# A routed FFN on one NeuronCore: the last four of 56 tiles put behind a branch on the number of tiles in use

## The chip, the cores and the metric

The kernel runs on one core of a Trainium2 chip. The metric is the device time of one execution in microseconds, as the median of several runs; lower is better. A profile is one further execution, recorded by the hardware profiler. Its line numbers are those of the kernel before, unless a line says otherwise.

## What is computed

Two layers of a graph network follow each other, each made of a graph convolution and a feed-forward part, over 6250 nodes of 256 features. The change lies in the feed-forward part of the first layer, a mixture of eight experts with two chosen per token:

```python
logits = xt @ Wr + br
probs = softmax(logits)
top_p, top_idx = top_k(probs, 2)
weights = top_p / top_p.sum(axis=-1, keepdims=True)
xn = (xt - mu) * rsqrt(var + LN_EPS)
xe = xn[None] * ln_g[:, None] + ln_b[:, None]
h = gelu(einsum('end,edh->enh', xe, W1) + b1[:, None])   # D = 256, H = 1024
y = einsum('enh,ehd->end', h, W2) + b2[:, None]
out = (weights[:, :, None] * y_of_the_two_chosen).sum(axis=1)
```

All of it is float32. The part after it (the second layer's graph sum) starts from `x + out`.

## The kernel before

The 6250 tokens are padded to 6272, 49 blocks of 128, and each has two experts, so 12544 (token, expert) pairs are computed. `routed_ffn` (line 494) does it in three stages.

*Ranking* (lines 511 to 589). Every pair gets a place, sorted by expert. Each expert's places are rounded up to whole tiles of 256 (`TS`), and `end` (line 529) is the running sum of the experts' tiles, so its last column is the number of tiles in use. How many that is depends on the data; the program is built for the largest number possible:

```python
TT = (2 * NP + n_exp * (TS - 1)) // TS      # 56
```

`te` (line 542) holds each tile's expert, `gi` the rows to gather for each place, and `so` the row of the result table `tab_y` for each place. A place that holds no pair has an `so` far out of bounds, so its row is not written, and an unused tile takes the last expert's weights.

*Tiles* (lines 591 to 654). For each tile, `start_tile` (line 592) reads its expert from `te` into a register of SP, and starts the loads of that expert's parameters (`pa`), weights (`w1` and `w2`, 1 MB each) and bias (`bb`) on SP's queue, and two gathers of 128 tokens on POOL's (line 606). This runs two tiles ahead. `turn` (line 611) transposes the gathered rows on TensorE and applies the expert's layer norm on VectorE (line 618). The tile itself is 16 matmuls with `w1` (line 630), eight Gelus on ScalarE (633), 16 matmuls with `w2` (643) in two halves, each with an addition of the bias on VectorE (645) and a scatter to `tab_y` on POOL (646). In the profile each float32 matmul is two, each with a weight load of its own. The transposes of the next tile stand between a tile's two groups of matmuls.

Beside the tiles runs other work that the second layer needs: an iterator, `beside`, of which every tile draws four steps (line 651) and the end of the loop whatever is left (653). Its steps sort the second layer's edges (`sorted_edges`, line 1453) and prepare the runs of the graph sum (`runs_of`, line 1577). They use VectorE, TensorE for transposes, ScalarE for copies, and SP's queue for loads and stores, such as the edge weights (1592) and the products `wab_d` (1642).

*Gather-back* (lines 655 to 662). The table `tab_y` is loaded in seven pieces on SP's queue (658), and VectorE adds the two rows of each token, times their gates, to `X` (661, 98 operations). Then a branch on another flag (lines 2170 and 2172) leads into the second layer.

The order on each engine is the program's order of issue, slightly rearranged by the framework's scheduler; waits between engines are on semaphores that it places. When a pool is closed and its room is taken by the next, the next one's writers wait for the last readers. A branch is loaded and taken by each engine for itself: a register load, then a compare and branch.

Of the kernel before, what the change touches and what calls it, by code (L numbers as in the profile page):

```python
# [22 lines left out]
I32 = mybir.dt.int32  # L23
I16 = mybir.dt.int16
AF = mybir.ActivationFunctionType
OP = mybir.AluOpType
AX = mybir.AxisListType
PSUM = bass.MemoryType.PSUM
# [4 lines left out]
P = 128  # L33
# [14 lines left out]
def chunks(n, size):  # L48
    return [(i, min(size, n - i)) for i in range(0, n, size)]
# [22 lines left out]
def tile_kernel(ctx, tc, src_ins, out):  # L72
    nc = tc.nc
# [420 lines left out]
    def routed_ffn(keep, tab_x, sel, gates, par_d, pre, beside):  # L494
# [5 lines left out]
        n_exp, _, HD = W1.shape  # L500
        FC = HD // P
        TS = 2 * P
        TT = (2 * NP + n_exp * (TS - 1)) // TS
# [4 lines left out]
        gi = keep.tile([P, SC], I32, name="gi")  # L508
        so = keep.tile([P, SC], I32, name="so")
        te = keep.tile([P, TT], I32, name="te")  # L510
        with tc.tile_pool(name="rk", bufs=1) as p, tc.tile_pool(name="rkw", bufs=4) as wp, \
                tc.tile_pool(name="rk_ps", bufs=1, space=PSUM) as pp:
            inc = p.tile([P, NT, n_exp], F32, name="inc")
            for e in range(n_exp):
                nc.vector.tensor_tensor_scan(inc[:, :, e], sel[:, :, e], sel[:, :, e], 0.0,
                                             op0=OP.add, op1=OP.max)
# [7 lines left out]
            end = p.tile([P, n_exp], F32, name="end")  # L524
# [15 lines left out]
            tb = p.tile([P, TT], F32, name="tb")  # L540
            nc.vector.tensor_reduce(tb, ge, AX.X, OP.add)
            nc.vector.tensor_copy(te, tb)


            all_e = [P, NT, n_exp]
# [29 lines left out]
            for i in range(2 * NT):  # L575
# [5 lines left out]
                                        op0=OP.is_equal, op1=OP.mult)  # L581
# [6 lines left out]
            nc.vector.tensor_scalar(gi, lf, 0.0, None, op0=OP.max)  # L588
            nc.vector.tensor_single_scalar(gi, gi, 1, op=OP.arith_shift_right)

        with tc.tile_pool(name="ff", bufs=3) as fp, tc.tile_pool(name="ff_ps", bufs=2, space=PSUM) as pp:
            def start_tile(j):
                _, (e,) = nc.values_load_multi_w_load_instructions(
                    te[0:1, j:j + 1], engines=[mybir.EngineType.SP], min_val=0, max_val=n_exp - 1,
                    skip_runtime_bounds_check_because="a count of n_exp-1 comparisons on chip")
                pa = fp.tile([P, NPAR], F32, name="pa")
                nc.sync.dma_start(pa, par_d[bass.ds(e, 1)].rearrange("e p c -> p (e c)"))
                w1 = fp.tile([P, KD, HD], F32, name="w1")
                nc.sync.dma_start(w1, W1[bass.ds(e, 1)].rearrange("e (k p) f -> p (e k) f", p=P))
                w2 = fp.tile([P, FC, D], F32, name="w2")  # L600
                nc.sync.dma_start(w2, W2[bass.ds(e, 1)].rearrange("e (c p) d -> p (e c) d", p=P))
                bb = fp.tile([P, D], F32, name="bb")
                nc.sync.dma_start(bb, b2[bass.ds(e, 1)].to_broadcast([P, D]))
                xg = fp.tile([P, 2, D], F32, name="xg")
                for i in range(2):
                    nc.gpsimd.indirect_dma_start(  # L606
                        out=xg[:, i, :], out_offset=None, in_=tab_x,
                        in_offset=bass.IndirectOffsetOnAxis(ap=gi[:, 2 * j + i:2 * j + i + 1], axis=0))
                return pa, w1, w2, bb, xg

            def turn(pa, xg):
                pt = pp.tile([P, KD, TS], F32, name="pt", bufs=1)
                for k in range(KD):
                    for i in range(2):
                        nc.tensor.transpose(pt[:, k, i * P:(i + 1) * P], xg[:, i, k * P:(k + 1) * P], ident)  # L615
                xe = fp.tile([P, KD, TS], F32, name="xe")
                for k in range(KD):
                    nc.vector.tensor_scalar(xe[:, k], pt[:, k], pa[:, FC + k:FC + k + 1],  # L618
                                            pa[:, FC + KD + k:FC + KD + k + 1], op0=OP.mult, op1=OP.add)
                return xe  # L620

            ahead = [start_tile(j) for j in range(2)]
            xe = turn(ahead[0][0], ahead[0][4])
            for j in range(TT):
                pa, w1, w2, bb, _ = ahead.pop(0)
                hs = []
                for f in range(FC):
                    ph = pp.tile([P, TS], F32, name="ph", bufs=4)
                    for k in range(KD):
                        nc.tensor.matmul(ph, w1[:, k, f * P:(f + 1) * P], xe[:, k, :],  # L630
                                         start=(k == 0), stop=(k == KD - 1))
                    h = fp.tile([P, TS], F32, name="h", bufs=2 * FC)
                    nc.scalar.activation(h, ph, AF.Gelu, bias=pa[:, f:f + 1])
                    hs.append(h)
                if j + 2 < TT:
                    ahead.append(start_tile(j + 2))
                if j + 1 < TT:
                    xe = turn(ahead[0][0], ahead[0][4])
                y = fp.tile([P, 2, D], F32, name="y")
                for i in range(2):  # L640
                    py = pp.tile([P, D], F32, name="py")
                    for f in range(FC):
                        nc.tensor.matmul(py, hs[f][:, i * P:(i + 1) * P], w2[:, f, :],  # L643
                                         start=(f == 0), stop=(f == FC - 1))
                    nc.vector.tensor_add(y[:, i, :], py, bb)
                    st = nc.gpsimd.indirect_dma_start(
                        out=tab_y, out_offset=bass.IndirectOffsetOnAxis(ap=so[:, 2 * j + i:2 * j + i + 1], axis=0),
                        in_=y[:, i, :], in_offset=None, bounds_check=2 * NP - 1, oob_is_err=False)
                    tc.declare_no_dep(st.ins, group="tab_y", reason="each place has a row of its own")
                    tc.add_to_no_dep_group("tab_y", st.ins)  # L650
                for _ in range(4):
                    next(beside, None)
            for _ in beside:
                pass
        with tc.tile_pool(name="fy", bufs=2) as fp:
            for t0, n in chunks(NT, CH):
                y = fp.tile([P, CH, 2 * D], F32, name="yy")
                nc.sync.dma_start(y[:, :n], tab_y[2 * t0 * P:2 * (t0 + n) * P].rearrange("(t p k) d -> p t (k d)", p=P, k=2))
                for t in range(t0, t0 + n):
                    for k in range(2):  # L660
                        nc.vector.scalar_tensor_tensor(X[:, t, :], y[:, t - t0, k * D:(k + 1) * D], g2[:, t, k:k + 1],
                                                       X[:, t, :], op0=OP.mult, op1=OP.add)
# [20 lines left out]
    class Head:  # L683
# [25 lines left out]
        def ffn(self, keep, beside):  # L709
            routed_ffn(keep, self.tab_x, self.sel, self.gates, self.par_d, "L0_ffn", beside)  # L710
# [1514 lines left out]
```

## Time and profile before

| what | value |
|---|---|
| median of 3 runs (lowest, highest) | 7773.18 us (7765.84, 7774.26) |
| the profiled execution's own time | 7783.37 us |
| its span | 7781.5 us |
| mean granted TensorE clock | 0.717 of full speed |
| busy over the span: PE, VectorE, ScalarE, POOL | 49%, 57%, 15%, 53% |
| first and last matmul of line 630 | 2784.8 and 3621.9 us |
| first load of tab_y (line 658) | 3632.38 us |
| last weighted add (line 661) begins | 3687.1 us |

A row by stretch gives the stretch, its length, then the busy time and number of instructions of each engine (PE is TensorE's matmuls, PEld its weight loads, DVE VectorE, ACT ScalarE, POOL GpSimd), the granted clock, the DMA engines' busy share and what they moved. A row of the timeline gives start, length, engine, line, operation, output and input, and in brackets the idle time before and what ended it. A row of waits gives who waited for what: total time, times, longest. A row of one line's instructions gives their number and the shortest, middle and longest duration in ns. A row of a DMA queue gives packets, MB and share of the engines' time. SPq, PEldq and the like are the engines' sequencers.

### The profile page before, as it was taken

The numbers are of one execution on the slowest core, as the hardware profiler recorded it, in microseconds if no ns is written. First come the engines' busy times: TensorE is split into PE (matmuls) and PEld (weight loads), VectorE is DVE, ScalarE is ACT, GpSimd is POOL, SyncE is SP. The second block draws the span as 40 slices with busy tenths as digits, with TensorE's granted clock in tenths as the row PEclk, the third lists the DMA queues.
The fourth block names the chain that finished last, engine by engine and source line by source line (L and its number), as shares of the span: only waits on it lengthen the run. The fifth ranks groups of instructions, "written<-read, shape, count | busy, mean of one in ns | idle before, by whom it ended". The sixth has DMA issues, their size and how long they took to land. (4 is left out here: it accounts for less than half of the span.)

```text
span 7781.5 us, 62325 instructions
## 1 busy us (share of the span) xinstructions
PE 3827.1 (49%) x17463; PEld 2901.2 (37%) x17463; DVE 4464.9 (57%) x10655; ACT 1161.1 (15%) x2758; POOL 4096.1 (53%) x4320
## 2 busy tenths in 40 slices
PE   3345545555445599996135555655555651111111
PEld 2234434444334378885023333433343431111111
DVE  4345555555555673443566666776676615665666
ACT  2011111111111112321001222212221210000000
POOL 0666666666666322321566666666566445555552
PEclk9667777777777799998557777777777875555555
DMA  4444444444444245565433333333333212222221
GB/s 124 119 114 119 113 117 120 117 119 118 115 114 120 73 163 190 184 228 167 139 89 99 98 103 100 101 102 102 95 100 101 80 43 52 45 48 52 50 50 41
DMA packets 496232, 821.82 MB, mean 106 GB/s; under 512 B 143344, under 2 KB 315587, under 8 KB 495842
## 3 DMA queue, kind: packets, MB, share of 16 engines
q0 software_dynamic: 190880, 462.26, 22.4%
q1 hardware_dynamic: 292326, 343.79, 14.5%
q10 hardware_dynamic: 12668, 11.68, 0.5%
q8 instruction: 141, 2.31, 0.1%
q14 instruction: 217, 1.78, 0.1%
HBM read 743.27 MB, written 77.29 MB: 105 GB/s over the span
## 5 line engine op out<-in xcount | busy, mean ns | idle before, releaser
L234 POOL DMA_INDIRECT g<-tab_ef,si x1616 | 1537.3, 951 | 995.4 <-issue 557.9
L1260 POOL DMA_INDIRECT g<-tab,si x1612 | 1539.6, 955 | 924.5 <-issue 577.4
L2028 DVE SCALAR_TENSOR_TENSOR run<-g,wab,run 128x256 f32<-128x256 f32 x2626 | 1264.9, 488 | 551.0 <-remote 179.2
L1260 POOL DMA_INDIRECT g<-tab_1f,si1s x787 | 761.8, 968 | 666.3 <-issue 587.1
L1363 PE MATMUL acc<-g,oh 128*128 128x264 f32 x3224 | 981.8, 465 | 174.6 <-issue 105.7
L1363 PEld LDWEIGHTS acc<-g,oh 128*128 128x128 f32 x3224 | 747.6, 238 | 365.0 <-issue 127.7
L1290 DVE TENSOR_REDUCE nd<-pd 128x64 f32<-128x192 f32 (+1 forms) x301 | 105.8, 352 | 1138.1 <-remote 914.2
L1714 PE MATMUL pf<-xt,w 128*128 128x512 f32 (+1 forms) x832 | 479.7, 715 | 474.9 <-issue 163.3
L2142 PE MATMUL acc<-run,oh 128*128 128x256 f32 x808 | 295.2, 500 | 628.3 <-DVE oh L2032 261.6
L1725 PE MATMUL pf<-w,h 128*128 128x256 f32 x1568 | 410.6, 412 | 183.1 <-ACT y L1730 80.9
L2142 PEld LDWEIGHTS acc<-run,oh 128*128 128x128 f32 x808 | 192.9, 251 | 730.4 <-issue 444.8
L1340 DVE TENSOR_TENSOR g<-g,mix 128x2048 f32<-128x2048 f32 x202 | 457.5, 2265 | 0.0
L1714 PEld LDWEIGHTS pf<-xt,w 128*128 128x128 f32 x832 | 179.7, 235 | 665.2 <-issue 321.6
L1363 PE MATMUL acc<-s,oh 128*128 128x72 bf16 x1267 | 96.6, 251 | 665.9 <-DVE s L1345 491.1
L1725 PEld LDWEIGHTS pf<-w,h 128*128 128x128 f32 x1568 | 316.3, 207 | 253.4 <-ACT y L1730 87.4
L1306 PE MATMUL zt<-ident,Z 128*128 128x128 f32 x228 | 76.6, 400 | 676.7 <-issue 380.2
L630 PE MATMUL ph<-xe,w 128*128 128x256 f32 x1792 | 405.4, 383 | 4.7 <-DVE xe L618 4.7
L643 PE MATMUL py<-w,h 128*128 128x256 f32 x1792 | 397.3, 379 | 0.0
L630 PEld LDWEIGHTS ph<-xe,w 128*128 128x128 f32 x1792 | 341.2, 192 | 51.4 <-DVE xe L618 5.7
L643 PEld LDWEIGHTS py<-w,h 128*128 128x128 f32 x1792 | 335.6, 190 | 43.1
L1363 PEld LDWEIGHTS <-oh 128*128 128x128 bf16 x1267 | 90.2, 133 | 669.9 <-issue 576.9
L606 POOL DMA_INDIRECT xg<-tab_x,gi x112 | 125.8, 1123 | 387.6 <-PE pt L615 313.1
(506 smaller groups left out, 5933.3 us busy)
## 6 DMA issues: line engine op xcount, KB each, us to landing
w<-in_L_ffn_W SPq DMA_DIRECT2D x112, 1024.0 KB
db<-s_d SPq DMA_DIRECT2D x299, 256.0 KB
g<-tab_ef,si POOLq DMA_INDIRECT x1616
g<-tab,si POOLq DMA_INDIRECT x1612
y_d<-y SPq DMA_DIRECT2D x196, 128.0 KB
yb<-y_d SPq DMA_DIRECT2D x49, 512.0 KB
g<-tab_1f,si1s POOLq DMA_INDIRECT x787
yy<-tab_y SPq DMA_DIRECT2D x7, 1792.0 KB
```

The source lines that it names most:

```text
L234: nc.gpsimd.indirect_dma_start(out=dst, out_offset=None, in_=table, in_offset=bass.IndirectOffsetOnAxis(ap=si[:, t:t + 1], axis=0))
L606: nc.gpsimd.indirect_dma_start(out=xg[:, i, :], out_offset=None, in_=tab_x, in_offset=bass.IndirectOffsetOnAxis(ap=gi[:, 2 * j + i:2 * j + ...
L630: nc.tensor.matmul(ph, w1[:, k, f * P:(f + 1) * P], xe[:, k, :], start=(k == 0), stop=(k == KD - 1))
L643: nc.tensor.matmul(py, hs[f][:, i * P:(i + 1) * P], w2[:, f, :], start=(f == 0), stop=(f == FC - 1))
L1260: nc.gpsimd.indirect_dma_start(out=g[:, j, :DH + H], out_offset=None, in_=tab, in_offset=bass.IndirectOffsetOnAxis(ap=si[:, t0 + j:t0 + j ...
L1290: nc.vector.tensor_reduce(nd[:, :n], pd[:, :n].rearrange("p j s d -> p j d s"), AX.X, OP.add)
L1340: nc.vector.tensor_mul(gh, gh, ps[0][:, o:o + n, :, None].to_broadcast([P, n, H, CD]))
L1363: nc.tensor.matmul(acc[b].rearrange("p s w -> p (s w)"), oh[:, t - a], m_, start=(t == lo), stop=(t == hi))
L1714: nc.tensor.matmul(ph[:, :n], w1[:, e, k, f * P:(f + 1) * P], xts[g][:, k, :n], start=(k == 0), stop=(k == KD - 1))
L1725: nc.tensor.matmul(py[:, :D], hs[g, e, f][:, j * P:(j + 1) * P], w2[:, e, f, :], start=(f == 0), stop=(f == FC - 1))
L2028: nc.vector.scalar_tensor_tensor(at[:, i] if j < Q - 1 else r[i], g[:, j, :], w, at[:, i], op0=OP.mult, op1=OP.add)
L2142: nc.tensor.matmul(acc[i], oh[:, k], r[k], start=(q % 2 == 0 and k == 0), stop=(last and k == 1))
```

## The change

The tile loop becomes a function `run_tiles(fp, pp, first, end, beside)`. It is called for the tiles 0 to 51 with the work beside, and a second time, inside a branch and with pools of its own, for the tiles 52 to 55 with an empty iterator. Within each call the loads run two tiles ahead, but not across the calls. The flag `more` is computed once, in the ranking stage: it is 1 if the number of tiles in use is over 52. `TM` is 56 - 8 // 2 = 52.

```diff
+        TM = TT - n_exp // 2
+        more = keep.tile([P, 1], I32, name="more")
...
             nc.vector.tensor_copy(te, tb)
+            nc.vector.tensor_scalar(more, end[:, n_exp - 1:], float(TM) + 0.5, None, op0=OP.is_gt)
...
-        with tc.tile_pool(name="ff", bufs=3) as fp, tc.tile_pool(name="ff_ps", bufs=2, space=PSUM) as pp:
+        def run_tiles(fp, pp, first, end, beside):
...
-            ahead = [start_tile(j) for j in range(2)]
+            ahead = [start_tile(j) for j in range(first, min(first + 2, end))]
             xe = turn(ahead[0][0], ahead[0][4])
-            for j in range(TT):
+            for j in range(first, end):
...
-                if j + 2 < TT:
+                if j + 2 < end:
                     ahead.append(start_tile(j + 2))
-                if j + 1 < TT:
+                if j + 1 < end:
                     xe = turn(ahead[0][0], ahead[0][4])
...
+        def ff_pools():
+            return tc.tile_pool(name="ff", bufs=3), tc.tile_pool(name="ff_ps", bufs=2, space=PSUM)
+
+        a, b = ff_pools()
+        with a as fp, b as pp:
+            run_tiles(fp, pp, 0, TM, beside)
+        used = nc.values_load(more[0:1, 0:1], min_val=0, max_val=1,
+                              skip_runtime_bounds_check_because="a comparison: 0 or 1")
+        with tc.If(used == 1):
+            a, b = ff_pools()
+            with a as fp, b as pp:
+                run_tiles(fp, pp, TM, TT, iter(()))
```

In the built program each engine has, behind tile 51, a register load of `more`, a compare and branch, the body, and a skipped side on which it brings its semaphores to the values that the body would have left (POOL first waits there for its scatters to land, SP for its loads). Line numbers behind the change move by 4 within the loop (630 becomes 634) and by 16 after it (658 becomes 674).

## The prediction

> **What bounds the kernel now.** I read the page first. Its chain of waits, followed back from the end, lies in the last layer (its longest pieces start at 6675 us), so it says nothing of this stage; the routed FFN's place has to be read from the stage itself. The instructions of line 630, the tiles' first matmul, run from 2784.8 to 3621.9 us. So next came the busy time by stretch, cut at the starts of the tiles (tile 52's first matmul is at 3572.50):
>
> ```profile
> core 0: us, PE busy (x) PEld busy (x) DVE busy (x) ACT busy (x) POOL busy (x), PEclk, DMA share, GB/s
> 3572.50:3586.75 14.25, 14.25 (x69) 12.55 (x68) 1.84 (x4) 3.79 (x8) 1.99 (x2) 1.00 0.49 159
> 3586.75:3601.00 14.25, 14.25 (x69) 12.55 (x68) 1.84 (x4) 3.79 (x8) 1.97 (x2) 1.00 0.26 83
> 3601.00:3615.26 14.26, 14.26 (x70) 12.55 (x69) 1.85 (x4) 3.79 (x8) 1.97 (x2) 1.00 0.01 2
> 3615.26:3632.38 17.12, 13.97 (x65) 11.97 (x63) 1.27 (x3) 3.80 (x8) 2.96 (x3) 1.00 0.01 0
> 3632.38:3687.64 55.26, 0.00 (x0) 0.00 (x0) 39.95 (x98) 0.00 (x0) 0.00 (x0) 0.50 0.69 232
> ```
>
> Tiles 52 to 55 take 14.25 us each. PE is busy for all of that at full clock; VectorE works 1.84 us of it, ScalarE 3.79 us. So PE alone sets these tiles' time. The last row is the weighted gather-back of the results: no PE, ScalarE or POOL work at all. Everything later waits for it, so time taken out before 3632 moves the rest of the program by the same amount.
>
> What starts that last stretch? The waits of SP's queue, and the timeline:
>
> ```profile
> SPq L658 <- DMA tab_y<-y,so: 43.9, 2, 27.8
> ```
>
> ```profile
> 3573.40 1.00 POOL L646 DMA_INDIRECT tab_y<-y,so  x1 [2.44 <-DVE y L645]
> ...
> 3629.97 0.98 POOL L646 DMA_INDIRECT tab_y<-y,so  x1 [2.47 <-DVE y L645]
> 3632.38 41.50 SPq L658 DMA_DIRECT2D yy<-tab_y  x7
> ```
>
> The first load of tab_y (line 658) waits for the scatters' landing: 3632.38 is 2.41 us after the last scatter was issued. Tile 51's second scatter is at 3573.40.
>
> Last, are the four tiles empty? By count of bytes, in the DMA view for 3583 to 3597 us (tile 52's two scatters), 3597 to 3611 (53's) and 3611 to 3632 (54's and 55's), the queue of gathers and scatters moved:
>
> ```profile
> q0 software_dynamic: 96, 0.00, 0.4%
> ...
> q0 software_dynamic: 192, 0.00, 0.6%
> ```
>
> The first line answers for each of the first two stretches, the second for the last. All eight scatters wrote nothing: their places are out of bounds. So at most 52 tiles hold rows. Counting the router's choices in the reference agrees: 1523, 1438, 1734, 1454, 2085, 1428, 1240 and 1598 tokens per expert, rounded up to 256, are 6+6+7+6+9+6+5+7 = 52 tiles. The flag will be 0 and the branch skipped.
>
> **Part by part.**
>
> *Tiles 52 to 55 gone from the run path.* After the change tile 51 (first matmul at 3558.24) ends as tile 55 ends now (first matmul at 3615.26): no transposes for a next tile, y's second half 7.11 us after the second matmul group starts, then the scatter. The shift is 3615.26 - 3558.24 = 57.02 us, four times 14.25. Their loads (2 MB of weights each), gathers and empty scatters go too. They lay beside PE and are worth nothing more.
>
> *The work beside.* Sorting and run steps are drawn four per tile until they run out. I count 172 steps of sorting and 34 of runs, 206, against 52 x 4 = 208 draws. So they end within tile 51, and the instruction order of the two builds agrees: VectorE has the same steps in the same places, with only tiles 52 to 55 taken out. Their last stores are issued at 3560.83 and 3561.97; each is 296 KB. At the 232 GB/s of the row above that is 1.3 us, so they land long before 3575. Cost nothing; the cover is tile 51's own PE work, and if one step slipped past it, VectorE's last products (1.22 us each) would be exposed.
>
> *The loads that PE waits for.* In the PE waits there is one of 5.6 us, at 3537 to 3542.7, for the edge weights, shortly before tile 51. Tile 52's weights were loading then, so taking them away could shorten it. But the edge weights were issued at 3523.6 and those weights at 3527.8 and 3533.9, behind them; and from 3539.8 to 3541.4 the DMA view shows 13 packets, 0.05 MB, one at a time: one engine working off a list of its own. I take 0, with 5.6 us of further gain as the end.
>
> *The flag.* One VectorE operation on 128x1 at the ranking stage, where VectorE is the busy engine: the 128x1 rows there are 0.14 to 0.15 us. Cost 0.15 us.
>
> *The skip itself.* The trace has one branch of this kind, at line 2172: register load 0.27 to 0.32 us, compare and branch 0.03 to 0.06 us on each engine. Each engine does it in its own queue; no barrier is in the order. PE's sequencer ran 4 us ahead of its matmuls there (load at 3625.3, last matmul ending 3629.2), and SP and ScalarE are done early, so theirs is hidden. POOL's load and branch (0.36 us) come behind the last scatter's issue, ending near 3573.9, and lie within the scatter's landing. But on the skipped side POOL waits for all its scatters to land and then raises their counters for the instructions not run, and SP's first load waits for those: a new hop. The nearest row, the raising of such counters (INC_SWDGE_SEM), has 109 to 591 ns, middle 338. SP also has more semaphores to wait through, 28 ns each, some 0.2 us. Together 0.15 + 0.34 + 0.2 = 0.7 us at the least.
>
> What a jump costs beyond that the trace shows only for far ones, at the end of the long branch of line 2172: VectorE's branch is at 7775.8 and its next record at 7778.7, ScalarE's at 7771.0 and 7773.6, so 2.6 to 2.9 us; PE's took 5.46 us by its own row:
>
> ```profile
> L2172 ACTq COMPARE_BRANCH  x2: 34/36/38, 3622.8 to 7771.0; - x2
> L2172 PEldq COMPARE_BRANCH  x2: 63/2762/5462, 3625.7 to 7764.2; - x2
> ```
>
> By these rows POOL would jump from 3574.3 to 3577.2, past the landing at 3575.4: about 1.9 us more, 2.6 in all. PE would be ready at 3568.7 + 5.5 = 3574.2, still hidden. [...]
>
> *Sum.* -57.0 + 1.5 = -55.5 us. The profiled execution took 7783.37 us (span 7781.5 and 1.9 around it), so the same execution changed would take 7727.9. The median of the runs is 7773.18, 10.2 lower; on it the forecast is 7717.7 us.
>
> **Rivals.**
>
> 1. *More than the tiles:* the edge weights were slowed by tile 52's loads, and PE's 5.6 us go too. For it: the wait ends only when those loads have drained. Against it: the order of issue. 7717.7 - 5.6 = 7712.1 us. Chance 0.08.
>
> 2. *The jump stalls in full, on several engines in turn:* a POOL stall of 2.9 us, then VectorE or SP stalling once more before the first weighted add: 2.6 + 2.9 = 5.5 us of cost, a gain of 51.5, 7721.7 us. For it: the far rows. [...] Chance 0.12.
>
> 3. *Slower: the branch is taken.* If 53 tiles are in use, the place is the restart of the pipeline. The second set of pools takes over the first's room, so tile 52's loads can't be issued until tile 51's scatter has landed, at 3575.4, instead of two tiles ahead. At the FFN's start the trace prices such a cold start: first load issued at 2774.10, first matmul at 2784.8, 10.7 us. Tile 52 would begin near 3575.4 + 1 + 10.7 = 3587.1 instead of 3572.5: 14.6 us lost and nothing saved, 7787.8 us, and over 0.2% slower with a far jump's stall. It decides from one row in a 53rd tile on. Expert 0 has 1523 tokens, 13 short of its sixth tile's end, and the 22 padding rows also choose; but the empty scatters show that they don't fill a seventh. Chance 0.02.
>
> 4. *It doesn't do what it says:* the work beside or a store spills past tile 51 and takes the place of the PE time. The gain would fall to that of the tail, below 0.2%, 7760 us or more. The order of instructions speaks against it. Chance 0.02.
>
> **Numbers.** The forecast itself has 0.76. Its own range, from costs of 0.7 and 2.6 us, is 7717 to 7719; rivals 1 and 2 reach 7712 and 7722; three runs before spread over 8.4 us, so I add that on the low side and on the high side: 7704 to 7730. About 0.2%, 15 us, is what a measurement of this kernel can tell from no change; only rivals 3 and 4 come near. Faster 0.96, same 0.02, slower 0.02.
>
> **What would show it.** In the changed profile: line 634 with 1664 matmuls instead of 1792; no gap over 15 us between tile 51's last scatter and the first load of tab_y, but about 3 to 4 us (2.41 now); the weighted adds still 98 in some 48 us; PE's wait for the edge weights still near 5.6 us; the stages after the FFN all as long as before. It is wrong if POOL or SP shows a gap of many microseconds behind the compare and branch, if tile 51 ends later than about 15 us after its first matmul, or if loads of weights appear after the branch.

## The result and the profile after

| | before | changed |
|---|---|---|
| median of 6 runs each (lowest to highest) | 7771.56 us (7765.84 to 7786.3) | 7731.24 us (7716.07 to 7744.22) |
| profiled execution: its time, span | 7783.37, 7781.5 us | 7720.16, 7718.4 us |
| start to the first tile's first matmul | 2784.8 us | 2772.0 us |
| from there to the first load of tab_y: the stage | 847.6 us | 787.3 us |
| from there to the end | 4149.1 us | 4159.1 us |

The ratio is 0.994, 95% interval 0.9923 to 0.9957, so 33 to 60 us less; the medians are 40.3 us apart. The forecast of -55.5 us is a ratio of 0.9929, inside that interval near its end. Its range of 7704 to 7730 us, of 7773.18, is 0.9911 to 0.9944 and holds the ratio, while the median of 7731.24 us lies 1.2 us above it. The two profiles are 63.1 us apart. 60.3 of that lies in the stage that was changed; the stages ahead of it came out 12.8 us shorter and those behind it 10.0 us longer.

First the line of the tiles' first matmul, in the profile after (number of instructions, shortest, middle and longest ns, first and last start):

```profile
L634 PE MATMUL ph<-xe,w x1664: 379/379/795, 2772.0 to 3547.3; 128*128 128x256 f32 x185
```

1664 instead of 1792: 128 fewer, four tiles of 32. So the branch was skipped. The same stage by stretch, cut at tile 51's start, at the end of its work and at the end of the gather-back:

```profile
core 0: us, PE busy (x) PEld busy (x) DVE busy (x) ACT busy (x) POOL busy (x), PEclk, DMA share, GB/s
3540.58:3557.71 17.13, 13.98 (x66) 11.98 (x64) 4.53 (x6) 4.70 (x9) 3.78 (x3) 0.97 0.14 50
3557.71:3613.80 56.09, 0.00 (x0) 0.00 (x0) 39.51 (x98) 0.00 (x0) 0.00 (x0) 0.50 0.67 229
```

The first row looks as tile 55's did: 13.98 us of PE in a stretch of 17.1. The second is the gather-back, still 98 weighted adds and 39.5 us of VectorE. Between the two is the hop that the skip adds: the time by which the branch delays the first load of tab_y behind the last scatter. The timeline, with tile 51's first matmul group, its two scatters, the first load of tab_y and the first weighted adds:

```profile
3540.58 7.07 PE L634 MATMUL ph<-xe,w 128*128 128x256 f32 x32
...
3551.85 0.98 POOL L650 DMA_INDIRECT tab_y<-y,so  x1 [8.98 <-DVE y L649]
3555.30 0.98 POOL L650 DMA_INDIRECT tab_y<-y,so  x1 [2.47 <-DVE y L649]
3559.30 41.63 SPq L674 DMA_DIRECT2D yy<-tab_y  x7
3567.27 11.42 DVE L677 SCALAR_TENSOR_TENSOR X<-yy,g,X 128x256 f32<-128x256 f32 x28 [12.25 <-DMA yy<-tab_y]
```

From the last scatter to the first load it is 4.00 us (2.41 before): the hop costs 1.59 us. Tile 51's last scatter comes 14.72 us after its first matmul. What the sequencers did at the branch (line 667) stands in that line's rows:

```profile
L667 PEldq COMPARE_BRANCH  x1: 3499/3499/3499, 3551.5 to 3551.5; - x1
L667 DVEq COMPARE_BRANCH  x1: 78/78/78, 3555.4 to 3555.4; - x1
L667 POOLq COMPARE_BRANCH  x1: 53/53/53, 3555.8 to 3555.8; - x1
...
L667 POOLq EVENT_SEMAPHORE  x4: 17/43/1967, 3556.0 to 3558.1; - x4
...
L667 POOLq INC_SWDGE_SEM  x1: 530/530/530, 3558.2 to 3558.2; - x1
```

VectorE and POOL branch in 53 to 78 ns, SP in 55 and ScalarE in 50; their next records stand 0.2 us (POOL) to 0.6 us (VectorE) behind. Only PE stalls, 3.5 us, and it has nothing left to do. POOL's long wait for the landing begins at 3556.0 and ends at 3558.0, 2.7 us after the last scatter's issue. In the kernel before it was SP that waited there, and its wait ended 2.1 us after its last scatter's issue (2.1 also in the kernel without a branch, below). Two more short waits and a gap take POOL 0.2 us, the counter 0.53 us, and SP's semaphores then 0.6 us to the load, where 0.3 us of them stood behind the landing before. So the hop of 1.6 us is a landing seen 0.6 us later, 0.2 and 0.5 us on POOL and 0.3 us more on SP, and no jump.

Last, the waits of PE in the stage (who waited for what: total us, times, longest). Before, then after:

```profile
PE pt_s L1602 <- DMA B<-in_edge_weight: 5.6, 1, 5.6
PE ph L630 <- DVE xe L618: 4.7, 2, 4.1
PE pt_s L1108 <- DVE bad L1098: 2.8, 1, 2.8
```

```profile
PE ph L634 <- DVE xe L622: 4.3, 2, 3.7
PE pt_s L1618 <- DMA B<-in_edge_weight: 2.9, 1, 2.9
PE pt_s L1124 <- DVE bad L1114: 2.6, 1, 2.6
```

The forecast had the wait for the edge weights stay at 5.6 us. It is 2.9.

### The profile page after: what moved, and what is told of

Its sections match the earlier page's. It is cut to its first block, busy times and chain, and to the rows that moved or that the text cites. A ratio compares the mean times of both kernels' runs of the same rounds, so it can differ in the third digit from the quotient of the medians.

```text
span 7718.4 us, 61635 instructions
## 1 busy us (share of the span) xinstructions
PE 3777.0 (49%) x17191; PEld 2850.5 (37%) x17191; DVE 4457.0 (58%) x10640; ACT 1144.0 (15%) x2726; POOL 4068.6 (53%) x4304
## 5 line engine op out<-in xcount | busy, mean ns | idle before, releaser
L634 PE MATMUL ph<-xe,w 128*128 128x256 f32 x1664 | 376.5, 383 | 4.3 <-DVE xe L622 4.3
L647 PE MATMUL py<-w,h 128*128 128x256 f32 x1664 | 369.0, 379 | 0.0
L634 PEld LDWEIGHTS ph<-xe,w 128*128 128x128 f32 x1664 | 316.4, 192 | 47.4 <-DVE xe L622 5.3
L647 PEld LDWEIGHTS py<-w,h 128*128 128x128 f32 x1664 | 311.7, 190 | 39.9
```

## The experiments

They ran on three chips, each beside runs of the kernel before: 7788.04 us on the first, 6489.48 on the second, 6481.26 on the third. The stage of this change is alike in the two profiles of the kernel before (847.6 us, and 846.7 on the second chip); on the third chip that kernel was timed but not profiled, so stages there are compared with the 846.7 us. The chips differ in stages the change doesn't touch: the second graph's gathers took 2422.1 us in the first profile of the kernel before and 2027.5 us on the second chip. On the first chip those stages also vary from profile to profile: 2399 to 2439 us for these gathers, over kernels that are the same there. So the stage's length and the two other chips carry most of what follows.

**The changed kernel again** (no edit).

> The changed kernel once more, unaltered. Theory A (the stage gained 60 us, and the smaller 40 us of the medians comes from stages that the change doesn't touch, which vary by 10 to 20 us from execution to execution): from the FFN's first matmul to the first load of tab_y again 786 to 789 us, from there to the end anything from 4145 to 4175 us, and the time in 7716 to 7744 us, in both of the groups seen so far. Theory B (the branch costs 15 to 20 us in some executions): the FFN stage itself is then 800 to 810 us in a run near 7741 us.

Measured: 7730.2 against 7788.04 us, ratio 0.9923 (0.9895 to 0.9951), 57.8 us less. The stage is 792.9 us, above the 786 to 789 expected and far from the 800 to 810 of theory B. Edge-weight wait 2.3 us.

**The four tiles left out, without branch or flag.** Tiles 52 to 55 are not computed at all here; with these inputs they hold no row. The edit is to the kernel before:

```diff
+            TU = TT - n_exp // 2
...
-            for j in range(TT):
+            for j in range(TU):
...
-                if j + 2 < TT:
+                if j + 2 < TU:
...
-                if j + 1 < TT:
+                if j + 1 < TU:
```

> The loop ends at tile 52 with no flag, no branch and no second copy of the tiles (it computes the four last tiles of no data, as long as 52 are enough). Theory A: the gap from the last scatter's issue to the first load of tab_y is 2.4 us again instead of 4.0, the rest as in the changed kernel, so the time is 1.6 us below it, which the runs can hardly tell. Theory B: the runs lose their upper group, and the median falls by 10 us or more below the changed kernel's, to about 7718 us.

Measured: 7740.07 us, ratio 0.9943 (0.9924 to 0.9962); stage 792.5 us, last scatter to first load 2.4 us. The hop of 1.6 us is gone. The time doesn't resolve it on this chip.

**The branch taken.** The flag is made 1 always, so the second call runs.

```diff
-            nc.vector.tensor_scalar(more, end[:, n_exp - 1:], float(TM) + 0.5, None, op0=OP.is_gt)
+            nc.vector.tensor_scalar(more, end[:, n_exp - 1:], -0.5, None, op0=OP.is_gt)
```

> The flag's comparison is with -0.5, so the branch is always taken and the four empty tiles run. By the rival of the prediction: tile 52's first matmul comes 10.7 + 1 us after tile 51's scatters have landed, so the FFN stage is 14.6 us longer than in the kernel before, about 862 us, and the time about 7786 us. If the pools' room doesn't hold the loads back, they are ahead and the stage is about 848 us as before.

Measured: 7787.63 us, ratio 1.0012 (0.9993 to 1.0031), but the stage is 861.2 us, 13.6 more than before. The timeline around tile 51's end:

```profile
3553.20 0.98 POOL L650 DMA_INDIRECT tab_y<-y,so  x1 [2.47 <-DVE y L649]
3556.09 0.35 SPq L601 DMA_DIRECT2D pa<-par_d  x1
...
3563.31 0.45 PE L619 MATMUL pt<-ident,xg 128*128 128x128 f32 x1 [10.85 <-issue]
...
3569.95 8.25 PE L634 MATMUL ph<-xe,w 128*128 128x256 f32 x32
```

Tile 52's loads start only when tile 51's scatter has landed (3556.09), and its first matmul comes 13.9 us after that. This is the restart of rival 3.

**All 56 tiles computed, but without loads for the last four.** They compute with tile 51's weights, parameters and biases instead of their own; their gathers stay, and their rows are empty. The edit is to the kernel before:

```diff
             def start_tile(j):
+                if j >= TT - n_exp // 2:
...
+                    return held[-1] + (xg,)
```

> The kernel before, with all 56 tiles computed, but tiles 52 to 55 load no weights, parameters or biases and use those of tile 51 (no place of theirs is in use). Theory PE (the tiles' time is TensorE's alone): the FFN stage is as before, 847 us, but for PE's wait for the edge weights, 5.6 us before, which falls to about 2.9 us as in the changed kernel if tile 52's loads caused the difference, and stays at 5.6 us if not. Rival DMA (the loads held the tiles up): the stage is 10 us or more shorter.

Measured: 7778.78 us, ratio 0.9996 (0.9975 to 1.0017); stage 850.0 us against 847.6. The edge-weight wait fell from 5.6 to 3.5 us, and the wait for VectorE's tile bad rose from 2.8 to 5.1 us (that one is 2.6 in one and 5.2 in another profile of kernels alike at this place, so it is scatter). So the loads alone gain nothing that can be measured. Yet they do lengthen the edge-weight wait: it is 5.3 to 5.6 us in the three profiles where tile 52's loads were issued ahead of it, and 2.3 to 3.5 us in the eight where they were not and that load was left as it is.

**The kernel before, once more, on the second chip.**

> The kernel before once more, for a second profile of it. Theory A (the stages that the change doesn't touch vary from execution to execution, and within the FFN stage only PE's stalls beside the sort's end and the granted clock after them vary): FFN stage 845 to 851 us; the stages up to the FFN and after it anywhere within 20 us of the first profile's. If instead the FFN stage varies as much as the rest, the difference of 60.3 us between the two first profiles is worth little.

Measured: 6489.22 against 6489.48 us, ratio 0.9999 (0.999 to 1.0007). Stage 846.7 us.

**Half the dose: two tiles behind the branch.**

```diff
-        TM = TT - n_exp // 2
+        TM = TT - n_exp // 4
```

> The branch of the changed kernel set two tiles later (TM = 54), so that tiles 52 and 53 are computed and only 54 and 55 are skipped. Theory PE: 2 x 14.25 us less than the kernel before and 1.6 us of hop, so an FFN stage of 847.6 - 28.5 + 1.6 = 820.7 us, or up to 5 us less by PE's stalls. Rival (the gain is in what is loaded or in the order, not in the number of tiles): a stage near 790 or near 847 us.

Measured: 6460.65 us, ratio 0.9954 (0.9941 to 0.9968), 28.8 us less; stage 821.9 us, 24.8 less than before. Two tiles are 28.5 us; the hop is 1.2 us (3.6 against 2.4). Here tile 52 is loaded as before, and the edge-weight wait is 5.6 us as before. PE jumps over half as many instructions, and its stall nearly goes:

```profile
L667 PEldq COMPARE_BRANCH  x1: 363/363/363, 3171.8 to 3171.8; - x1
```

**The changed kernel with loads of 73 rows split in 64 and 9.** The sorting loads its last chunk as 73 rows of 4 KB. By the bytes moved in the profile of before, from 3535 to 3542.7 us, cut in 40 slices, the edge weights trickle in, and PE starts again when they end:

```profile
GB/s 144 32 80 202 154 250 325 255 117 112 165 319 367 378 383 351 367 372 362 356 362 410 250 112 32 64 21 21 21 21 43 21 21 21 43 73 119 112 164 193
```

A slice is 0.19 us; 21 GB/s in it is 4 KB, about one row per slice, where all transfers together reach 350 GB/s and more before. Cut finer, from 3539.8 to 3541.4 us, a row comes every 0.16 us, and the 16 DMA engines are 7% busy, as much as 1.1 of them. Not every load of the kind goes so slowly: of the two loads of in_src (line 1592), the one of 128 rows (512 KB) was issued at 3448.6 and VectorE's wait for it ended at 3453.6, 5.0 us later; the one of 73 rows (292 KB) was issued at 3477.9, and the wait ended at 3497.1, 19.2 us later. So I guessed at the number of rows, and that 64 and 9 as two loads would go faster; no trace had shown it.

```diff
-            nc.sync.dma_start(dst[:full], ap[c * P * F:(c * P + full) * F].rearrange("(r e) -> r e", e=F))
+            even = full // 16 * 16
+            for r0, r1 in ((0, even), (even, full)):
+                if r0 < r1:
+                    nc.sync.dma_start(dst[r0:r1], ap[(c * P + r0) * F:(c * P + r1) * F].rearrange("(r e) -> r e", e=F))
```

The first edit acts on two loads of 73 rows, the edge weights and the edges' sources (in_src). A third load, 74 rows of s_dst, is split in the same way into 64 and 10.

> The changed kernel, with each load of 73 or 74 rows of 4 KB in the preparation of the runs made as two: 64 rows, and the rest. Theory of one engine (a load of 73 rows goes to one DMA engine, and PE's wait for the edge weights is that engine's list): the wait, 2.3 to 5.6 us so far, is gone, the load lands within about 6 us of its issue instead of 16 to 19, and the FFN stage is 2 to 5 us shorter than the changed kernel's, 783 to 790 us. Rival (it waits for the weights' traffic): the wait stays above 2 us.

Measured: 6420.81 us, ratio 0.9893 (0.9878 to 0.9908), 68.7 us less than before. Stage 782.5 us. The edge-weight wait is gone from the list, and the wait for xe is 0.6 us. That one came from the sources' load: VectorE, which makes xe, stood 13 us behind it in the kernel before:

```profile
3497.14 0.69 DVE L1611 CAST A<-A 128x1024 f32<-128x1024 int32 x1 [13.06 <-DMA A<-in_src]
```

Of the ratios this is the lowest, but its interval overlaps that of the changed kernel on the third chip (below), which was not timed on this one.

**The changed kernel on the third chip.**

> The changed kernel a third time, with the three below, for a comparison free of the graph stages' scatter (on the chip of the last three runs, the kernel before took 6489.5 us and scattered by a few us only). From the stage: 57.0 us of four tiles, less 1.6 us of hop, plus about 3 us of the wait for the edge weights, so 58 us below the kernel before on whichever chip it runs, and the FFN stage 788 us.

Measured: 6422.16 us, ratio 0.9908 (0.9893 to 0.9923), 59.1 us less; stage 790.1 us.

**Without branch, on the third chip** (the edit above).

> The loop that ends at tile 52 with no branch, again. The hop alone should tell it from the changed kernel: 1.6 us shorter, with a gap of 2.4 us between the last scatter and the first load of tab_y. If the branch has a cost elsewhere, the two differ by more than 4 us.

Measured: 6416.3 us, ratio 0.9903 (0.9887 to 0.9918), 65.0 us less; stage 785.5 us. The branch thus costs 5.9 us by the medians, more than the 1.6 us of its hop and more than the 4 us from which the expectation reads a cost elsewhere; one of the four times here, 6425.52 us, is above all four of the changed kernel. In the two profiles 4.6 us of the difference lie in the stage, 3.5 ahead of it, and -2.7 behind. The stage's part can be placed. Its rows for the same 100 us beside the sort (the granted clock is the third number from the end), with the branch and then without:

```profile
2984.90:3084.90 100.00, 91.56 (x431) 77.87 (x430) 42.69 (x57) 31.36 (x60) 23.46 (x25) 0.95 0.73 238
2981.40:3081.40 100.00, 92.03 (x445) 78.45 (x445) 43.11 (x58) 31.43 (x60) 24.45 (x26) 0.98 0.75 247
```

The clock took 100 x 0.03 = 3.0 us more in the first, and the hop 1.6, together 4.6. PE waited 2.9 us for the tile bad in both; with the branch the clock was 0.50 behind it (3013.1 to 3016.5), and without it 1.00 (3009 to 3016). That is over 100 us ahead of the branch. So no row puts more than the hop at the branch. On the first chip the same two kernels differed by 0.4 us in the stage.

**The branch taken, on the third chip** (the edit above).

> The branch always taken, again. From the first profile of it, an FFN stage of 861 us against 847: 14 us slower than the kernel before, by the restart of the pipeline (tile 52's first matmul about 16 us after tile 51's last one has ended, where none is lost before).

Measured: 6495.3 us, ratio 1.0021 (1.0012 to 1.003), 14.0 us more than before. Stage 866.8 us.

**The split alone, on the kernel before** (the edit above, without tiles left out).

> The kernel before, with only the loads of 73 and 74 rows made as two. The waits of PE for the edge weights (5.3 us) and for xe behind the sources' load (4.2 us) are gone, so the FFN stage is 837 us or a little more and the time 9 to 10 us below the kernel before. Added to the changed kernel the same edit is worth less, 6 to 7 us, since there tile 52's loads no longer lengthen the first wait: then e5's 68.7 us less is 58 and 7, and some 3 us remain for the clock.

Measured: 6464.93 us, ratio 0.9976 (0.9966 to 0.9986), 16.3 us less. Stage 834.1 us, 12.6 less than the 846.7 of the kernel before on the second chip. The PE waits in the stage, there and then here:

```profile
PE pt_s L1602 <- DMA B<-in_edge_weight: 5.3, 1, 5.3
PE ph L630 <- DVE xe L618: 4.8, 2, 4.2
```

```profile
PE pt_s L1108 <- DVE bad L1098: 3.0, 1, 3.0
...
PE ph L630 <- DVE xe L618: 0.6, 1, 0.6
```

Waits of 5.3 us, and of 4.2 us for xe, went, 9.5 in all, but the stage lost more. The rest shows in the granted clock. By stretch, the last 138 us of sorting beside the tiles, in the kernel before on the second chip and then in this one (columns as above):

```profile
2990.70:3090.70 100.00, 90.59 (x440) 77.19 (x439) 43.00 (x58) 31.55 (x60) 26.33 (x27) 0.98 0.76 242
3090.70:3128.70 38.00, 32.08 (x152) 27.42 (x151) 7.43 (x13) 12.36 (x21) 7.98 (x8) 0.91 0.53 156
```

```profile
2984.70:3084.70 100.00, 95.14 (x472) 81.55 (x471) 44.56 (x61) 33.72 (x63) 28.30 (x29) 1.00 0.79 258
3084.70:3122.70 38.00, 37.40 (x186) 32.50 (x185) 11.36 (x18) 15.09 (x28) 9.10 (x9) 1.00 0.67 205
```

Before, the clock is 0.98 and 0.91: 100 x 0.02 + 38 x 0.09 = 5.4 us of full speed lost, part of it while PE stood still anyway. With the split it is 1.00 throughout. So here the stalls cost their length and then some clock: by these numbers 9.5 us at the least and 14.9 at the most, and 12.6 were measured. The second row bears this out in all 13 profiles: it is 0.91 in the three with an edge-weight wait of 5.3 to 5.6 us, 0.96 in the eight with 2.3 to 3.5 us, and 1.00 in the two without one. The first row is less steady, 0.93 to 1.00, and 0.97 in the other profile with the split.

## Why the prediction came out as it did

**Four tiles of 14.25 us.** Right. The stage lost 60.3 us in the first pair of profiles and 54.7 to 60.3 us in all three profiles of the changed kernel (847.6 less 792.9 and 787.3; 846.7 less 790.1, on another chip, is 56.6). Half the tiles gave 24.8 us against 28.5 less the hop, 27.3. That PE and not the loads sets these tiles' time is shown by the kernel without their loads: computing them costs the full stage, 850.0 us.

**The skip, 1.5 us.** The size is right, at 1.59 us, but by luck. No run shows the 1.5 us of the sum, a figure between 0.7 us without a jump's stall and 2.6 us with one; the runs showed a hop of 1.59 us, and of 1.2 with two tiles behind the branch. No stall of 2.9 us showed on POOL and VectorE (branches of 53 and 78 ns, the next record 0.2 and 0.6 us behind), so rival 2 falls, and the lower end should have held. What was too small there is the rest: 0.34 us for the counter and 0.2 us for SP, 0.54 in all, where the hop is 1.59. The counter took 0.53 us and SP's semaphores 0.3 us more than before; that POOL sees the landing 0.6 us later than SP did, and spends 0.2 us more behind it, was not in the sum. PE's 3.5 us were hidden, as argued. The branches over bodies of 16 to 36 instructions took under 0.08 us, PE's over some 540 took 3.5 us (tiles 52 to 55 are 273 matmuls and 268 weight loads in the profile before), and over half as many 0.36. Why PE's took so much longer was not shown.

**The loads that PE waits for, taken at 0.** This step failed, and it is the term of the sum that was mis-sized. The argument was the order of issue: the edge weights were queued ahead of tile 52's weights. But the edge weights' 73 rows came one at a time. At the measured 0.16 us a row they would need 11.7 us alone; from their issue to the end of PE's wait it took 19.1 us before (3523.6 to 3542.7) and 16.3 after (3509.1 to 3525.4). As I read it, they went through one engine (1.1 of the 16 were busy) and shared it with tile 52's rows; the sharing itself was not measured. Taking those loads away shortened the wait by 2.1 to 3.3 us in every profile (from 5.3 and 5.6 us to 2.9, 2.3 and 2.4; 3.5 without the loads alone). With it the stage's sum is -57.0 + 1.6 - 2.7 = -58.1 us, against 60.3 measured. The rest is about what the clock took. The same 138 us, before and then after:

```profile
3414.80:3514.80 100.00, 91.23 (x443) 77.59 (x441) 42.98 (x59) 31.89 (x60) 25.86 (x27) 0.98 0.76 242
3514.80:3552.80 38.00, 31.79 (x149) 27.09 (x148) 7.69 (x13) 12.36 (x21) 7.18 (x8) 0.91 0.53 157
```

```profile
3402.00:3502.00 100.00, 92.29 (x446) 78.50 (x446) 43.10 (x58) 31.46 (x60) 24.78 (x26) 0.98 0.76 247
3502.00:3540.00 38.00, 34.53 (x164) 29.45 (x163) 7.73 (x13) 12.35 (x21) 3.93 (x4) 0.96 0.24 70
```

By the count used above 5.4 us were lost before and 2.0 + 1.5 = 3.5 after, 1.9 less, which makes -60.0. In the changed kernel's two other profiles the first row is 0.93 and 0.95, and the clock took 3.1 and 1.1 us more than before; the same sums give -55.6 and -57.2, against 54.7 and 56.6 measured. So the wait's 3 us are in every pair, while the clock's part changes its sign. Rival 1 was half right: about 3 us of the 5.6.

**Everything later moves by the same amount.** Right in the stage, and blurred in the time. On the two other chips, where the later stages are steady, the change gives 59.1 us, and half the dose 28.8. In the first result 40.3 us remain, and 57.8 in the repeat on the first chip. Between these two nothing of the stage differs by that much (787.3 and 792.9 us). What does are the gathers before and behind it, by 10 to 20 us from profile to profile. The smaller gain of the first result is put down to them; since only one execution of each set was profiled, it isn't shown for the others.

**Rival 3, the branch taken.** It did not happen here, with 52 tiles in use, but its price was right: 14.6 us were forecast, 14.0 measured on the third chip (interval 8 to 19 us), 13.6 and 20.1 in the stage. That is luck in part. The cold start was sized from the FFN's start at 10.7 us and took 13.9, so that tile 52's first matmul came 17.7 us later behind tile 51's last scatter than before (16.8 us after it, where it was 0.9 us ahead). Against this PE's wait for the edge weights was 3.3 us shorter (2.3 against 5.6), since tile 52's loads were not there yet.

**Rival 4.** It fell: the stage ends with tile 51, and the last weighted adds are the same 98.

What stays open: why the same 2.9 us of waiting is followed by half the clock in one profile and by the full clock in another, and why the gathers of the graph stages take 2399 to 2439 us on one chip and 2023 to 2028 on the others.

## What to carry to other kernels

Work on empty data was worth its time on the bounding engine here, 57.0 us of PE, and some 3 us more for a wait that its loads had lengthened: read the first from the stretches of the stage, and ask what else the loads share. A skipped branch was cheap here, 1.2 to 1.6 us: its skipped side puts a hop between the last transfer ahead of it and its reader. The taken side restarts the pipeline, 13.9 us from its first load to its first matmul of line 634; one row too many here turns 59 us of gain into 14 of loss. And order of issue didn't protect a load whose rows came one by one, every 0.16 us: look for loads that, like the 73 rows here (19.2 us against 5.0 for 128 rows), take longer than their size explains.

## What was not expected of the hardware

A load of 73 rows of 4 KB trickled at one row per 0.16 us, and splitting three such loads was worth 16.3 us by itself (interval 9 to 22; 12.6 in the stage), about a tile. PE's jump over some 540 instructions took 3.3 to 3.7 us in four profiles, and 0.36 over half as many, while the branches of the other engines took under 0.08, with the next record at most 0.6 us behind. And a stall of PE in a busy stage left the granted clock over the 38 us around it at 0.91 when it was 5.3 to 5.6 us long, and at 0.96 when it was 2.3 to 3.5.
